# A four-layer decoder on one core: maxima turned and picked on chip in the fifth sublayer, and forty blocks of later keys and values among its first forty units

## The chip, the core and the metric

The kernel runs on one core of one Trainium2 chip, as one launch. The metric is the device time of that launch in microseconds (us), taken as the median of several runs. The engines are named as the profile names them: PE is the matrix engine (PEld its weight loads), DVE the vector engine, ACT the scalar engine, POOL the GpSimd engine, and SP the queue that issues nearly all DMA transfers. Each engine works through its own instructions in a fixed order and waits on semaphores for the others.

## What is computed

The reference is a decoder of four layers with three sublayers each, on 64 sequences of 64 tokens with 256 features (4096 tokens), all in f32. After each sublayer the result is added to x and normalized. Two sublayers bear on the change. The fifth is a cross attention with eight features to a head:

```python
# x and context, 64 x 64 x 256, are taken as 64 sequences of 8 heads x 8 rows x 256 columns
qk = einsum('bhdq,bhdl->bhql', qh, kh) * scale      # scores
sm = softmax(qk, axis=-1)
ret = einsum('bhql,bhdl->bhdq', sm, vh)
x = layernorm(x + gamma * ret)
```

The softmax needs the maximum of each row of scores. The eleventh sublayer is a cross attention whose keys and values are products of the context with two weights of 256x512; the context is an input, so these products depend on nothing that the earlier sublayers compute:

```python
k = (context @ Wk + bk)     # 4 heads of 128
v = (context @ Wv + bv)
```

## The kernel before

The tokens are held on chip as 32 tiles of 128 tokens in eight groups of four (TG = 4). The sublayers run one after the other; `self.ring` is a ring of eight weight slots of 1 MB each that all of them draw on in order.

**The fifth sublayer** is `l1_xattn`. It walks the 32 tiles in 34 steps, and each step in four units, one for each j, so there are 136 units. A unit has two halves, each a call of `scored`. In a step, `new` is the tile whose scores are formed for the first time, only to find the row maxima, and `old` is the tile two steps behind, whose scores are formed again, transposed, and go through the exponential. In a half, PE computes for `old` two banks `sk` and for `new` one tile `sq`. The operands of these products have 32 rows and lie in four groups of 32 partitions, two for `new` and two for `old`; the profile shows them as 32\*128. DVE takes the negated maxima of `sq` into `mc` (L1563). The maxima of `old` are brought into the banks `sk` ahead of the scores by a product with ones (L1551), so that the exponential on ACT (L1569) has nothing to subtract. `weighted` then multiplies the exponentials `e` with the values `vt` (L1600): the first half of a unit is followed by the second part of the unit two back, and the second half by the first part of the unit one back. The banks `sk` come from a ring of three, on which also the blocks `kv` and the turned maxima `mt` draw; the tiles `e` come from a ring of ten.

**The maxima's way.** After the first unit of a step, `move(turn)` deals with the tile whose maxima were finished in the step before. PE turns `mc` (L1575), ACT copies the high part (L1577), DVE forms the low part (L1578), SP writes both to DRAM (L1580) and reads two rows of each group of partitions back into `mx` (L670). `scored` needs `mx` at the start of the following step.

**The later keys and values.** `ContextRows` holds a list of blocks: one for the keys and one for the values of each chosen tile. `fill(n)` takes the next n blocks: two products of 128x128 by 128x512 on PE (L170; the profile shows four instructions), one copy of 128x512 on ACT (L174) and one write of 256 KB to DRAM on SP (L175). Before, 19 tiles are chosen, so there are 38 blocks: ten in the first ten units of the fifth sublayer, in whose code their results take a tile of the ring `e`; 21 around the end of the eighth sublayer; seven at the start of the ninth, in `Linear.first` (`fill(5)` and `fill(2)`). In the eleventh sublayer (`l3_xattn`), `ready` tells whether a tile was chosen. If so, its keys and values are loaded from DRAM and get their bias on POOL; otherwise PE forms them (L2143) and DVE adds the bias (L2604). The order of work on PE, DVE, ACT and POOL there is written out by hand in `l3_attentions`, together with the twelfth sublayer's.

**The sixth sublayer's weights.** `first.load()` takes four ring slots and loads three weights of 1 MB. Before, it stands ahead of the loop over the steps. From unit 48 on, one part of the list `ahead` runs in each unit: thirteen parts that form signs (POOL and DVE), seven that quantize the first group's rows, and then `first.turn`, with products and transposes of 128x128 on PE (L268, L273).

**Other parts of the stage.** `load` brings in a tile's operands, 1 MB in eight transfers, at the end of a step for the step after the next one. `store` writes results; after the last tile of a group four parts of `later` follow: a reciprocal and a scaling on DVE (L1634, L1635), loads, sums on POOL, and a normalization whose statistics are on DVE (L582, L585).

## Time and profile before

Three runs took 4292.81, 4290.98 and 4278.38 us; the median is 4290.98 us. The execution that was profiled took 4279.01 us, of which its span, from the first instruction to the last, is 4277.3 us.

| stretch of the span, us | what runs | length | PE busy | DVE busy | ACT busy | POOL busy | granted clock |
|---|---|---|---|---|---|---|---|
| 641 to 684 | fifth sublayer, units 0 to 9 | 43 | 34.48 | 27.81 | 15.23 | 9.35 | 0.87 |
| 684 to 817 | units 10 to 39 | 133 | 129.69 | 79.02 | 76.02 | 16.95 | 0.54 |
| 817 to 1239 | units 40 to 135 | 422 | 418.09 | 257.99 | 245.39 | 109.42 | 0.53 |
| 1934 to 1990 | end of the eighth, start of the ninth | 56 | 46.49 | 41.10 | 32.31 | 4.07 | 0.98 |
| 3250 to 4277 | eleventh and twelfth | 1027 | 951.99 | 737.82 | 651.61 | 394.43 | 0.99 |

### The profile page before, as it was taken

To read this page: it belongs to the slowest core of one execution; us is meant where nothing else is said; L and a number is where in the kernel's file an instruction comes from. 1 tells how busy PE (TensorE), PEld (TensorE's weight loads), DVE (VectorE), ACT (ScalarE), POOL (GpSimd) and SP (SyncE) were. 2 spreads that over 40 slices of the span, in tenths; PEclk is the share of its full clock that TensorE was granted. 3 is DMA by queue.
4 is the path that set the end of the run, shared out by engine and by line. 5 is a ranking of instruction groups with operands and counts; after the bars stand their busy time and mean duration, and the time that the engine had idled before them with its cause. 6 is when DMAs were issued, how large, how long until landed. Compare 5 with 4: busy or idle time off the path is not lost.

```text
span 4277.3 us, 71626 instructions
## 1 busy us (share of the span) xinstructions
PE 4044.9 (95%) x27272; PEld 2584.3 (60%) x27272; DVE 2988.3 (70%) x5646; ACT 2299.4 (54%) x4649; POOL 1549.7 (36%) x1617
## 2 busy tenths in 40 slices
PE   8879888999999899998999999999999989999997
PEld 6646664444457555554666666666666667666765
DVE  6856655676658468887777777777766777777775
ACT  5545454565543456755444444444443466676765
POOL 4511121141234111112555555555554343444432
PEclk9989996555579999999999999999999999999999
DMA  2211213434330000013111111111112110010000
GB/s 82 71 54 45 60 53 112 130 106 132 93 88 1 12 1 1 1 42 102 31 26 28 28 26 31 26 30 26 26 31 87 55 31 27 24 29 22 27 25 13
DMA packets 137307, 195.60 MB, mean 46 GB/s; under 512 B 22464, under 2 KB 89728, under 8 KB 135552
## 3 DMA queue, kind: packets, MB, share of 16 engines
q1 hardware_dynamic: 136000, 189.41, 16.0%
q8 instruction: 217, 3.56, 0.3%
q10 hardware_dynamic: 960, 1.57, 0.2%
q14 instruction: 130, 1.06, 0.1%
HBM read 100.47 MB, written 48.23 MB: 35 GB/s over the span
## 4 chain that ended last, share of the span: by engine, by line
PE 39%; DVE 9%; ACT 2%; issue 1%; POOL 1%; DVEq 0%; POOLq 0%; ACTq 0%
PE p L2143 18%; PE acc L2500 5%; PE acc L2766 4%; PE qT L562 2%; PE s L2438 2%; PE kT L562 1%; PE h L450 1%; PE y L2468 1%; PE yt L562 1%; DVE s L2699 1%; PE s L2692 1%; PE o L503 1%; PE pt L562 1%; DVE mxx L2701 1%; DVE s L2698 1%
## 5 line engine op out<-in xcount | busy, mean ns | idle before, releaser
L1563 DVE TENSOR_REDUCE mc<-sq 128x4 f32<-128x1024 f32 x256 | 310.8, 1222 | 174.6 <-PE sq L1558 161.4
L1569 ACT ACTIVATE e<-sk 128x512 f32<-128x512 f32 x512 | 278.1, 595 | 225.3 <-PE sk L1561 222.8
L556 POOL TENSOR_TENSOR rstd<-rstd,neg_half 128x1 f32<-128x1 f32 (+1 forms) x187 | 145.5, 778 | 588.0 <-DVE rstd L554 582.7
L556 POOL TENSOR_TENSOR hrq<-hrq,neg_half 128x4 f32<-128x4 f32 (+1 forms) x192 | 234.4, 1221 | 244.4 <-DVE hrq L554 238.2
L1600 PE MATMUL ret<-e,vt 128*32 128x256 f32 x2048 | 267.7, 616 | 1.4 <-ACT r L1605 1.4
L556 POOL TENSOR_TENSOR hrk<-hrk,neg_half 128x4 f32<-128x4 f32 x160 | 187.8, 1174 | 223.4 <-DVE hrk L554 173.7
L2143 PE MATMUL p<-l3a_wq,xt 128*128 128x512 f32 x512 | 243.8, 599 | 9.7 <-DVE v L543 8.4
L2143 PE MATMUL p<-l3a_wk,xt 128*128 128x512 f32 x512 | 247.9, 607 | 0.0
L2143 PE MATMUL p<-l3x_wq,xt 128*128 128x512 f32 x512 | 243.8, 599 | 0.8 <-DVE k L2604 0.8
L2766 PE MATMUL acc<-l3x_wo,yt 128*128 128x256 f32 x1024 | 235.0, 382 | 5.0 <-DVE yt L2750 3.5
L2143 PE MATMUL p<-l3a_wv,xt 128*128 128x512 f32 x512 | 233.2, 598 | 0.6 <-DVE k L543 0.4
L2500 PE MATMUL acc<-l3a_wproj,yt 128*128 128x256 f32 x1024 | 232.1, 379 | 0.7 <-DVE yt L543 0.7
L2500 PEld LDWEIGHTS acc<-l3a_wproj,yt 128*128 128x128 f32 x1024 | 194.2, 190 | 53.9 <-issue 29.2
L2766 PEld LDWEIGHTS acc<-l3x_wo,yt 128*128 128x128 f32 x1024 | 192.6, 191 | 40.8 <-ACT yt L2750 4.9
L1551 PE MATMUL sk<-mx,ones 2*128 2x512 f32 x512 | 201.1, 765 | 8.4 <-DMA mx<-l1x_m 6.6
L1558 PE MATMUL sq<-l1x 32*128 32x256 f32 x1024 | 191.4, 473 | 6.0 <-DVE mc L1563 5.8
L1551 PEld LDWEIGHTS sk<-mx,ones 2*128 2x128 f32 x512 | 73.5, 274 | 191.7 <-ACT e L1569 106.1
L562 PEld LDWEIGHTS qT<-ident,q 128*128 128x128 f32 x1024 | 121.5, 141 | 103.6 <-issue 76.4
L1561 PEld LDWEIGHTS sk<-l1x 32*128 32x128 f32 x1024 | 163.8, 315 | 19.7
L2484 POOL TENSOR_TENSOR hry<-hry,neg_half 128x8 f32<-128x8 f32 x64 | 106.2, 1659 | 179.1 <-DVE hry L2480 176.8
L562 PE MATMUL qT<-ident,q 128*128 128x128 f32 x1024 | 156.7, 276 | 11.7 <-DVE hlo L414 10.2
L1561 PE MATMUL sk<-l1x 32*128 32x256 f32 x1024 | 159.3, 401 | 0.0
(451 smaller groups left out, 10697.5 us busy)
## 6 DMA issues: line engine op xcount, KB each, us to landing
vs<-v SPq DMA_DIRECT2D x308, 128.0 KB
l1x<-l1x_c SPq DMA_DIRECT2D x128, 128.0 KB
l1x<-l1x_x SPq DMA_DIRECT2D x128, 128.0 KB
l3x_kv<-kv SPq DMA_DIRECT2D x38, 256.0 KB
k<-l3x_kv SPq DMA_DIRECT2D x19, 256.0 KB
v<-l3x_kv SPq DMA_DIRECT2D x19, 256.0 KB
x<-in_x SPq DMA_DIRECT2D x8, 512.0 KB
ct<-in_ctxT SPq DMA_DIRECT2D x8, 512.0 KB
```

The lines of the kernel that those rows point to most:

```text
L556: nc.gpsimd.tensor_tensor(out, out, self.neg_half[:, :n], ALU.pow)
L562: self.nc.tensor.transpose(ps[:, j * P : (j + 1) * P], blk, self.ident)
L1551: nc.tensor.matmul(ps, ones[rows], mx[old % 2][rows, j, :].unsqueeze(1).broadcast_to([2, 2, D]), start=True, stop=False)
L1558: nc.tensor.matmul(sq[:, k, n, :], x_[rows, j, part], c_[rows, j, :], start=True, stop=True)
L1561: nc.tensor.matmul(ps[:, n, :], c_[rows, j, part], x_[rows, j, :], start=False, stop=n == 1)
L1563: nc.vector.tensor_reduce(mc[new % 2][:, ra : ra + 2, 2 * j : 2 * j + 2], sq, AX.X, ALU.max, negate=True)
L1569: nc.scalar.activation(es[rb + k], ps, AF.Exp, scale=scale)
L1600: nc.tensor.matmul(ret[32 * r : 32 * r + 32, :], vt[i % 2][:, lc, 4 * j + r, :], es[r][:, lc, :], start=lc == 0, stop=lc == 1,)
L2143: self.nc.tensor.matmul(ps, lhs(c), w(c, cols), start=c == 0, stop=c == 1 and bias is None)
L2484: nc.gpsimd.tensor_tensor(r, r, self.neg_half[:, :8], ALU.pow)
L2500: nc.tensor.matmul(acc[:, :D], yts[h % 2][:, h // 2, :], wp[n // 8][:, (n % 8) * D : (n % 8 + 1) * D], start=n == 0, stop=n == 15,)
L2766: nc.tensor.matmul(acc[:, :D], yts[h % 2][:, h // 2, :], w.o[n // 8][:, (n % 8) * D : (n % 8 + 1) * D], start=n == 0, stop=n == 15,)
```

## The change

The maxima stay on chip. After the first unit of a step, DVE copies `mc` into the first eight columns of `mh` (rounded to the form that PE reads in one pass) and writes what was lost by the rounding into the next eight; PE turns `mh`, and ACT copies the result to `mt`. In `scored`, four products of 32 rows by 256 columns, two for each bank, take the place of two products of two rows by 512 columns: `pick` holds ones in the rows that belong to one column of maxima, so the product adds the high and the low part. The transfers through DRAM go, four for each tile. Of the later keys and values 31 tiles are chosen, all but the first, so there are 62 blocks: 40 in the first 40 units of the fifth sublayer, 21 around the end of the eighth as before, and one at the start of the ninth. `first.load()` moves into unit 41, as one of its slots is that of the blocks' weight; the list `ahead` is filled there and still starts at unit 48.

```diff
--- before.py
+++ after.py
@@ -148,7 +148,7 @@
     def __init__(self, dec):
         self.dec = dec
         tiles = [(g, t) for g in range(dec.n_groups) for t in range(TG)]
-        tiles = [tile for k, tile in enumerate(tiles) if k >= 3 and (k % 2 or k % 6 == 2)]
+        tiles = tiles[1:]
         self.dram = {}
         for g, t in tiles:
             for i in range(2):
@@ -1512,21 +1512,24 @@
         both = [self.weight(f"l1x{i}", F32R).rearrange("p (i n) -> p i n", i=2) for i in range(NB)]
         xr, cr = ([w[:, i].rearrange("p (j c) -> p j c", j=4) for w in both] for i in range(2))
         vt = [wk.tile([P, 2, 16, 32], F32, tag=f"vt{i}", name="vt", bufs=1) for i in range(2)]
-        mc = [wk.tile([P, 4, 32], F32, tag=f"mc{i}", name="mc", bufs=1) for i in range(2)]
-        mx = [wk.tile([P, 4, D], F32R, tag=f"mx{i}", name="mx", bufs=1) for i in range(2)]
-        ones = wk.tile([P, P], F32R, tag="ones", name="ones", bufs=1)
-        nc.scalar.activation(ones, self.ident, AF.Identity, bias=1.0, scale=0.0)
+        mc = [wk.tile([P, 4, 8], F32, tag=f"mc{i}", name="mc", bufs=1) for i in range(2)]
+        mh = [wk.tile([P, 4, 32], F32R, tag=f"mh{i}", name="mh", bufs=1) for i in range(2)]
+        mt = [wk.tile([P, P], F32R, tag=f"mt{i}", name="mt", bufs=1) for i in range(2)]
+        rows_of = wk.tile([P, 8], F32, tag="rows_of", name="rows_of", bufs=1)
+        pick = wk.tile([P, 8, P], F32R, tag="pick", name="pick", bufs=1)
+        of = self.ident.rearrange("p (r k n) -> p n r k", r=4, k=4)
+        nc.vector.tensor_reduce(rows_of, of[:, :, :, :2], AX.XY, ALU.add)
+        nc.gpsimd.tensor_copy(pick, rows_of.unsqueeze(2).broadcast_to([P, 8, P]))
         for t in vt:
             nc.gpsimd.memset(t, 0.0)
             nc.gpsimd.memset(t[:, :, :, 8:9], 1.0)
-        for t in mc:
-            nc.vector.memset(t, 0.0)
+        for t in mh:
+            nc.gpsimd.memset(t.bitcast(F32), 0.0)
 
         dram = lambda name, shape: [
             self.tc.dram_tile(shape, F32, name=f"l1x_{name}{g}") for g in range(self.n_groups)
         ]
         rd, sd, qd = (dram(n, [NTOK, D]) for n in "rsq")
-        md = [[self.tc.dram_tile([P, P], F32, name=f"l1x_m{h}{i}") for i in range(NB)] for h in range(2)]
         state = {}
 
         def load(g, t):
@@ -1544,13 +1547,15 @@
             for k in range(2):
                 if old is not None:
                     sks.append(bank("sk"))
-            group = lambda r, n=32: slice(32 * r, 32 * r + n)
+            group = lambda r: slice(32 * r, 32 * r + 32)
             ra, rb = 2 * half, 2 - 2 * half
-            for k, ps in enumerate(sks):
-                rows = group(rb + k, 2)
-                nc.tensor.matmul(
-                    ps, ones[rows], mx[old % 2][rows, j, :].unsqueeze(1).broadcast_to([2, 2, D]), start=True, stop=False
-                )
+            for n in range(2):
+                for k, ps in enumerate(sks):
+                    rows = group(rb + k)
+                    nc.tensor.matmul(
+                        ps[:, :, n * P : (n + 1) * P], pick[rows, 2 * j + n, :],
+                        mt[old % 2][rows].unsqueeze(1).broadcast_to([32, 2, P]), start=n == 0, stop=False,
+                    )
             for n in range(2):
                 part = slice(n * P, (n + 1) * P)
                 for k in range(2 if sq is not None else 0):
@@ -1571,17 +1576,12 @@
 
         def move(i):
 
+            m, h = mc[i % 2], mh[i % 2]
+            nc.vector.tensor_copy(h[:, :, :8], m)
+            nc.vector.tensor_tensor(h[:, :, 8:16], m, h[:, :, :8].bitcast(F32), ALU.subtract)
             ps = bank("mt")[:, 0, :P]
-            nc.tensor.transpose(ps, mc[i % 2].rearrange("p r n -> p (r n)"), self.ident)
-            hi, lo = (wk.tile([P, P], F32R, tag=tag, name=tag, bufs=1) for tag in ("mhi", "mlo"))
-            nc.scalar.copy(hi, ps)
-            nc.vector.tensor_tensor(lo, ps, hi.bitcast(F32), ALU.subtract)
-            for h, mt in enumerate((hi, lo)):
-                nc.sync.dma_start(out=md[h][i % NB], in_=mt.bitcast(F32))
-                self.load(
-                    mx[i % 2][h:P:32].bitcast(F32).rearrange("r j q -> r (j q)"),
-                    md[h][i % NB].rearrange("(r n) q -> r (n q)", r=4)[:, : 8 * P],
-                )
+            nc.tensor.transpose(ps, h.bitcast(F32).rearrange("p r n -> p (r n)"), self.ident)
+            nc.scalar.copy(mt[i % 2], ps)
 
         def values(g, t):
             v = vt[t % 2]
@@ -1661,8 +1661,7 @@
         load(*tiles[1])
         engines = {mybir.EngineType.PE, mybir.EngineType.Activation, mybir.EngineType.DVE}
         before, behind, turn, wait, units = None, None, None, 0, 0
-        first.load()
-        ahead = first.weights() + first.quantize(0) + [lambda: first.turn(0, bank("xt"), bank("rows"))]
+        ahead = []
         with self.tc.manual_schedule(engines=engines):
             for step in range(n + 2):
                 new = step if step < n else None
@@ -1680,7 +1679,7 @@
                     if before is not None:
                         weighted(*before, 0)
                     behind = before
-                    if units < 10:
+                    if units < 40:
                         self.context.fill(
                             1, wk, "e", 10, 0, nc.scalar.copy, lambda: bank("kv").rearrange("p i n -> p (i n)")
                         )
@@ -1692,6 +1691,10 @@
                             later.pop(0)[1]()
                             wait = 0
                     units += 1
+                    if units == 42:
+                        first.load()
+                        ahead += first.weights() + first.quantize(0)
+                        ahead.append(lambda: first.turn(0, bank("xt"), bank("rows")))
                     if units > 12 * TG and ahead:
                         ahead.pop(0)()
                     before = (old, j, es) if old is not None else None
```

## The prediction

> **What bounds the kernel now.** PE is busy 95% of the span, so I look for where its time is dear. The page's rows by slices, with the busy times above them:

> ```profile
> PE 4044.9 (95%) x27272; PEld 2584.3 (60%) x27272; DVE 2988.3 (70%) x5646; ACT 2299.4 (54%) x4649; POOL 1549.7 (36%) x1617
> ...
> PEclk9989996555579999999999999999999999999999
> ```

> The clock is halved in slices 6 to 10: the fifth sublayer, 641 to 1239 us. The answer by stretches (columns as in the front) shows PE full there, at half clock:

> ```profile
> 850.00:900.00 50.00, 50.00 (x417) 24.27 (x409) 35.89 (x44) 29.46 (x56) 28.82 (x23) 0.50 0.43 120
> ...
> 950.00:1000.00 50.00, 46.09 (x463) 23.76 (x461) 34.16 (x31) 32.57 (x63) 6.69 (x10) 0.73 0.52 138
> ```

> In 950 to 1000 the clock was high for a while. PE's timeline there:

> ```profile
> 966.49 0.64 PE L1600 MATMUL ret<-e,vt 128*32 128x256 f32 x8
> 967.05 0.68 PE L1551 MATMUL sk<-mx,ones 2*128 2x512 f32 x2
> ...
> 968.48 0.61 PE L1551 MATMUL sk<-mx,ones 2*128 2x512 f32 x2
> ...
> 972.89 0.50 PE L1551 MATMUL sk<-mx,ones 2*128 2x512 f32 x2 [2.69 <-DMA mx<-l1x_m]
> ```

> and in the steady state:

> ```profile
> 861.63 0.79 PE L1551 MATMUL sk<-mx,ones 2*128 2x512 f32 x2
> ...
> 863.79 0.79 PE L1551 MATMUL sk<-mx,ones 2*128 2x512 f32 x2
> ```

> A half takes 2.16 us at half clock, 1.42 at full. A step of eight halves and the turning (0.41 us, 1030.16 to 1030.57) takes 17.69 or some 11.7. The maxima's way through DRAM took 12 us (turned at 960.75, there at 972.89): hidden at half clock, late by 2.69 us at full. That wait costs the clock: by slices of 3.4 us it is 1.00 up to 973.3 and 0.50 after it; at 693.4, behind a wait of 2.47 us on the same transfer, it falls too. It came back at 949.4, when `first.turn` had sent products of 128x128 through PE.

> **An area count** (mine, from the rows) fits these turns. A 32x128 product fills a quarter of the array, one of 128x32 too. A 256-column pass takes 0.11 us at full clock in the scores; the f32 instructions of L170 take 0.43 for 512 columns (17.43 us for 40), which I count as two passes. A half then holds 512 array columns of scores and 1024 of `ret`; a window of 3.41 us has 8190. Windows at full clock that kept it held 0.38 or more, those that lost it 0.37 or less; the steady half clock holds 0.26 to 0.34 and never recovers; the lowest that recovered held 0.40. So I put the limit at 0.37 to 0.40.

> [...]

> **Units 0 to 9:** ten blocks as before; the wait of 1.48 us on `mx` at 672.85 goes. **-1.5.**

> **Units 10 to 39**, 30 blocks more. Before: two units from 683.91 to 693.40, then seven steps of 17.69: 133.3 us. After, four passes of 429 ns in each unit keep the area above 0.4, so the clock stays full. The unit's length shows in unit 10 of before, which follows two units with blocks:

> ```profile
> 676.93 0.27 PE L1575 MATMUL mt<-ident,mc 128*128 128x128 f32 x1
> ...
> 683.91 0.50 PE L1551 MATMUL sk<-mx,ones 2*128 2x512 f32 x2
> ...
> 685.95 0.50 PE L1551 MATMUL sk<-mx,ones 2*128 2x512 f32 x1 [0.30 <-ACT e L1569]
> ...
> 687.18 0.61 PE L1551 MATMUL sk<-mx,ones 2*128 2x512 f32 x2
> ```

> It takes 3.27 us: with five tiles of `e` in a unit and ten in the ring, the first `e` of a unit takes the place of the one two units back, which PE reads only after this half, so ACT's exponentials wait for PE and PE's next bank for ACT. Behind that ACT wait stand only exponentials that are not ready either. The block adds 1.82 (675.11 to 676.93), the turning 0.26 in seven steps: 30 x 5.09 + 1.8 = 154.5. **+21.** ACT's added copy (585 ns) fits into 5.1 us; if not, PE waits for banks.

> **Units 40 to 135.** The turning now waits for DVE: the last maxima come from the previous step, but DVE's copy and difference stand behind the reduce of the half just run. Steady row:

> ```profile
> 1028.00 0.79 PE L1551 MATMUL sk<-mx,ones 2*128 2x512 f32 x2
> ...
> 1030.16 0.48 PE L1575 MATMUL mt<-ident,mc 128*128 128x128 f32 x1
> ```

> ```profile
> 1029.07 1.22 DVE L1563 TENSOR_REDUCE mc<-sq 128x4 f32<-128x1024 f32 x1 [0.94 <-PE sq L1558]
> 1030.97 0.29 DVE L1578 TENSOR_TENSOR mlo<-mt,mhi 128x128 fp32r<-128x128 f32 x1 [0.68 <-ACT mhi L1577]
> ```

> The reduce ends at 1030.29; `sq` now follows two passes of `pick` instead of lying beside one, 0.21 later. The two small DVE operations aren't in the trace: the nearest are 128x4 ones, which follow each other by 0.21 when dependent (929.99, 930.20); 0.46 with the signal to PE. So PE turns at 1030.96 instead of 1030.16: 0.8 lost, in 23 steps **+18**. Bounds: nothing if the two are issued free of the reduce, 1.2 each (+28) if each takes the 0.29 of L1578 and more. Everything behind the turning on PE waits; ACT is then idle.

> At full clock the same wait is 1.2 us (0.66 + 0.57 of PE against 0.78 + 1.22 + 0.46 of DVE). A window holding it has (3.41 - 1.2 - 0.26) / 1.42 halves, each now 1792 columns with `pick`'s 256, and 256 of the turning: 0.33; split over two windows 0.37 to 0.43. By phase about one step in four falls below the limit. Group parts on DVE (1.73 + 0.45 us at 1048.87, 2.3 us at 1008.20) against a slack of some 0.9 (a reduce ends 0.67 + 1.22 after its half begins, and its tile is needed after two halves, 2.84) break it more surely; the first, for group 1, is in unit 44. So I expect the full clock to last about five units past the fill, 1.4 us each (4.32 less 2.9): **-7.** After `first.turn` in unit 68 it returns for seven or eight units, as before. At half clock `pick` lifts the area to at most 0.36, short of 0.37.

> `pick` itself: bounds 0 (same columns; weight loads run ahead) and 0.1 to 0.2 for a half (one weight load, 181 ns at full clock): 0 to +40. I take 0, as the weight loads of L1561 lie beside matmuls. Making `pick`, `rows_of` and `mh` lies beside units 0 to 7. `first.load()` in unit 41 has seven units before its data is used; 3 MB at the 300 GB/s and more of 1246 to 1254 us need 10. It is queued ahead of tile 12's load, which has a step of 17 us. SP loses 128 transfers of the maxima, which nothing else waits for.

> **Start of the ninth:** six blocks fewer. PE's fifth ended at 1980.21, when the scaled rows were ready since some 1979.5: -0.7; but PE is emptier, and a further window at half clock costs up to 1.7. **+1.**

> **Eleventh sublayer:** twelve tiles less to form, 3.44 us of PE each. Between first score products (L2692), a prepared tile followed by a prepared one takes 29.3 us (tiles 13, 14, 19, 20, 26), an unprepared one 29.8 (12, 18, 22, 28), a prepared one followed by an unprepared 30.65. So each tile saves 1.8, not 3.44: the values' part gives nothing. POOL's added sums fit in (20 of 50 us busy). **-21**, bounds 0 and -41.

> **Sum:** -1.5 + 21 + 18 - 7 + 1 - 21 = +10.5 on 4279.0: 4290. The runs' median, 4291.0, lies 12 above this execution, of which I add half: **4296**.

> **Rivals.** *The clock holds past unit 40* because no transfer is waited for. For: 949 to 973 kept it through seven windows, and `pick` adds area. Against: the wait for DVE above. A step then takes 8 x 1.42 + 0.26 + 1.2 = 12.8 against 17.7; throughout, 23 x 4.9 = 113, in place of +18 - 7: 4171. Held half the way: about 4235. *The clock falls between the blocks*: in units 10 to 39 a `kv` copy waits on ACT for its tile's write (SP issues eight loads at 0.59 and, every fourth step, eight more writes ahead of it), PE stops for lack of banks, and a window without a block falls under 0.37. It decides once that wait exceeds about 1 us; a unit then takes 4.32 + 3.6, 2.8 more; in ten units +28: 4324. *The change moves less than it says*: the 22 blocks left are the 21 near the eighth's end and one more, so no.

> **Chances.** Forecast 0.50 (4275 to 4312), the clock holding 0.27 (4165 to 4265), falling 0.23 (4305 to 4340). A measurement tells 0.3% (13 us) from no change. Faster: 0.27 and 0.04 of the forecast; same: 0.31 of it; slower: 0.15 and 0.23. The range leaves out a tenth at each end: 4235 to 4326.

> **What would show it.** Right: units 10 to 39 at clock 1.0 and 5.1 us; half clock again from about unit 45; PE's turning waiting 0.8 us for DVE; tiles of the eleventh at 29.3. Wrong: a granted clock above 0.8 from 840 to 1180, or below 0.9 before; a turning without a wait.

## The result and the profile after

The changed kernel takes **4320.35 us** (median of four runs, 4307.69 to 4337.39), the kernel before 4284.68 in the runs beside them: a ratio of 1.0091, 95% interval 1.007 to 1.0112, slower by 36 us. The prediction was 4296 in a range of 4235 to 4326. The profiled execution took 4307.69 us, the fastest of the four; its span is 4306.0, 28.7 more than before's 4277.3. The prediction's +10.5 answers to these 28.7. Here and below a ratio leaves out runs that lie more than 1.5% above the fastest run of the same kernel (two of e8's four, one of e10's ten), while the medians keep them. The changed kernel's page, the rows that were shown of before:

```profile
PE 4002.1 (93%) x27764; PEld 2581.6 (60%) x27784; DVE 2989.1 (69%) x5653; ACT 2310.9 (54%) x4672; POOL 1581.4 (37%) x1644
...
PEclk9989999956659999999999999999999999999999
```

The clock is at 0.9 or more in two slices that stood at 0.6 and 0.5 before, PE is busy for 43 us less, and yet the span is longer: PE now waits. By stretches of the fifth sublayer (units 0 to 9, 10 to 39, 40 to 135; columns as in the front):

```profile
641.00:682.60 41.60, 31.10 (x166) 13.86 (x160) 28.37 (x40) 15.05 (x28) 8.29 (x14) 0.88 0.37 119
682.60:850.10 167.50, 147.89 (x1332) 69.92 (x1331) 79.78 (x85) 90.25 (x173) 19.92 (x24) 0.99 0.40 124
850.10:1276.80 426.70, 400.67 (x3824) 211.92 (x3827) 259.86 (x316) 244.87 (x462) 109.08 (x111) 0.57 0.39 110
```

Between the starts of units (of the last stretch up to unit 135, without the 4.3 us of that unit):

| part | before | after | difference | predicted |
|---|---|---|---|---|
| units 0 to 9 | 42.7 | 41.9 | -0.8 | -1.5 |
| units 10 to 39 | 133.4 | 167.5 | **+34.1** | +21 |
| units 40 to 135 | 416.7 | 422.4 | +5.7 | +18 - 7 |
| unit 135 to the eleventh's first score product | 2033.8 | 2034.1 | +0.3 | +1 |
| from there to the first one of tile 31 | 938.6 | 927.4 | **-11.2** | -21 |
| the rest (ahead of unit 0, and the tail) | | | +0.7 | |

**Units with a block** run at full clock, as foretold, but at 5.58 us instead of 5.09. One of them, timeline of the changed kernel:

```profile
779.05 1.02 PE L170 MATMUL kv<-l3x_wkv,ct 128*128 128x512 f32 x2
...
780.67 0.64 PE L1600 MATMUL ret<-e,vt 128*32 128x256 f32 x8
...
781.38 0.59 ACT L174 COPY kv<-kv 128x512 f32<-128x512 f32 x1 [2.93 <-PE ret L1600]
781.86 1.09 ACT L1574 ACTIVATE e<-sk 128x512 f32<-128x512 f32 x2
...
782.02 0.88 PE L1555 MATMUL sk<-mt,pick 32*128 32x256 f32 x3 [0.71 <-ACT kv L174]
```

The block's products end at 780.07, its copy starts at 781.38, 0.07 after `ret` has ended: its tile of the ring still held exponentials that `ret` reads. Meanwhile the bank stays full and PE waits 0.71. Nine of the 30 copies wait so, all 1.3 us behind their products. They are only a part of it: the 21 units whose copy comes in time take 5.53 on the average too. PE's waits over all 30 units (us in total, times, longest):

```profile
PE sk L1555 <- ACT kv L174: 7.7, 15, 0.7
PE sk L1555 <- ACT e L1574: 5.6, 13, 0.6
PE ret L1600 <- ACT r L1605: 4.6, 15, 0.4
```

The unit that the forecast was read from has the second of these waits (0.30), but neither the first nor the third, which stands in every second unit.

**The turning** waits for DVE, as foretold, 0.65 at half clock:

```profile
890.82 1.22 DVE L1568 TENSOR_REDUCE mc<-sq 128x4 f32<-128x1024 f32 x1 [0.94 <-PE sq L1563]
...
891.96 0.17 DVE L1580 CAST mh<-mc 128x32 fp32r<-128x32 f32 x1
892.17 0.32 DVE L1581 TENSOR_TENSOR mh<-mc,mh 128x32 fp32r<-128x32 f32 x1
892.63 0.45 PE L1583 MATMUL mt<-ident,mh 128*128 128x128 f32 x1 [0.65 <-DVE mh L1581]
```

Steps at half clock take 18.3 instead of 17.7. In unit 52 the wait is far longer, since a group's statistics, themselves waiting for POOL's sum, stand between on DVE:

```profile
908.75 0.43 DVE L582 BATCH_NORM_STATS2 bnst<-z 128x6 f32<-128x256 f32 x1 [2.65 <-POOL z L1648]
...
911.70 2.34 DVE L1568 TENSOR_REDUCE mc<-sq 128x4 f32<-128x1024 f32 x2
...
914.74 0.45 PE L1583 MATMUL mt<-ident,mh 128*128 128x128 f32 x1 [4.39 <-DVE mh L1581]
```

**In the eleventh** the steady tiles take 29.3 as foretold, but tile 0 takes 35.60 instead of 31.43. Among the waits of these 35.6 us are POOL's for the prepared keys of tile 1 to arrive and PE's for POOL (us in total, times, longest):

```profile
POOL k L2600 <- DMA k<-l3x_kv: 9.3, 1, 9.3
PE yt L562 <- POOL y L2489: 3.9, 1, 3.9
```

The second row, of the same answer, is what PE loses: 0.3 before. On POOL that `y` comes behind the sums for tile 1's keys and values.

### The profile page after: what moved, and what is told of

Its sections match the earlier page's. It is cut to its first block, busy times and chain, and to the rows that moved or that the text cites. A ratio compares the mean times of both kernels' runs of the same rounds, so it can differ in the third digit from the quotient of the medians.

```text
span 4306.0 us, 72512 instructions
## 1 busy us (share of the span) xinstructions
PE 4002.1 (93%) x27764; PEld 2581.6 (60%) x27784; DVE 2989.1 (69%) x5653; ACT 2310.9 (54%) x4672; POOL 1581.4 (37%) x1644
## 3 DMA queue, kind: packets, MB, share of 16 engines
q14 instruction: 129, 1.06, 0.1%
## 4 chain that ended last, share of the span: by engine, by line
PE 57%; DVE 17%; ACT 7%; issue 3%; POOL 2%; DMA 1%; SPq 0%; ACTq 0%; POOLq 0%; DVEq 0%
PE p L2146 16%; PE acc L2503 5%; PE ret L1600 4%; PE sk L1555 3%; PE acc L2769 3%; PE acc L1766 2%; DVE s L2702 2%; PE kv L170 2%; PE gate L1961 2%; PE s L2441 2%; PE qT L562 2%; PE up L1961 2%; PE sk L1566 1%; PE kT L562 1%; PE acc L1977 1%
## 5 line engine op out<-in xcount | busy, mean ns | idle before, releaser
L1600 PE MATMUL ret<-e,vt 128*32 128x256 f32 x2048 | 233.8, 543 | 7.2 <-ACT r L1605 7.2
L1555 PEld LDWEIGHTS sk<-mt,pick 32*128 32x128 f32 x1024 | 117.8, 258 | 189.8 <-ACT e L1574 94.9
L1555 PE MATMUL sk<-mt,pick 32*128 32x256 f32 x1024 | 191.2, 434 | 18.2 <-ACT kv L174 8.7
L1563 PE MATMUL sq<-l1x 32*128 32x256 f32 x1024 | 167.5, 420 | 7.5 <-DVE mc L1568 7.3
L2146 PEld LDWEIGHTS p<-l3a_wv,xt 128*128 128x128 f32 x512 | 92.1, 190 | 97.4 <-issue 82.0
L2417 POOL TENSOR_TENSOR k<-k,hrk 128x512 f32<-128x512 f32 x128 | 144.7, 1130 | 10.0
```

The lines of the kernel that those rows point to most:

```text
L1555: nc.tensor.matmul(ps[:, :, n * P : (n + 1) * P], pick[rows, 2 * j + n, :], mt[old % 2][rows].unsqueeze(1).broadcast_to([32, 2, P]), start ...
L1563: nc.tensor.matmul(sq[:, k, n, :], x_[rows, j, part], c_[rows, j, :], start=True, stop=True)
L1600: nc.tensor.matmul(ret[32 * r : 32 * r + 32, :], vt[i % 2][:, lc, 4 * j + r, :], es[r][:, lc, :], start=lc == 0, stop=lc == 1,)
L2146: self.nc.tensor.matmul(ps, lhs(c), w(c, cols), start=c == 0, stop=c == 1 and bias is None)
L2417: nc.gpsimd.tensor_tensor(k, k, wide(r, P), ALU.mult)
```

## The experiments

"Half" is the time at half clock between unit 10 and the start of unit 135, from the clock records of the profiled execution; 516.7 us before. The stretches are of the one execution that was profiled, the ratio is to the kernel before, run beside each; where two kernels are compared below, it is by what each differs from its own runs of before.

| kernel | median, us | ratio, 95% interval | units 10 to 39 | units 40 to 135 | half | eleventh |
|---|---|---|---|---|---|---|
| changed | 4320.35 | 1.0091, 1.0070 to 1.0112 | 167.5 | 422.4 | 367 | 927.4 |
| e1 turning only | 4296.49 | 1.0042, 1.0029 to 1.0054 | 124.4 | 439.8 | 520 | 938.7 |
| e2 blocks only | 4321.98 | 1.0103, 1.0086 to 1.0120 | 180.4 | 417.5 | 414 | 927.7 |
| e3 DVE's part first | 4233.29 | 0.9909, 0.9880 to 0.9937 | 174.2 | 337.4 | 147 | 927.3 |
| e4 own tiles | 4306.30 | 1.0065, 1.0048 to 1.0082 | 148.5 | 425.9 | 377 | 927.5 |
| e5 both mends | 4193.34 | 0.9780, 0.9757 to 0.9803 | 148.0 | 330.3 | 96 | 927.6 |
| e6 e3 with ten blocks | 4168.57 | 0.9712, 0.9676 to 0.9749 | 94.8 | 364.9 | 219 | 938.5 |
| e7 23 tiles | 4304.21 | 1.0048, 1.0030 to 1.0066 | 142.3 | 443.6 | 491 | 933.3 |
| e8 parts spread | 4220.20 | 0.9777, 0.9723 to 0.9832 | 94.7 | 419.7 | 402 | 941.0 |
| e9 full products | 4410.99 | 1.0294, 1.0276 to 1.0312 | 174.0 | 523.7 | 476 | 924.2 |
| e10 narrow products | 4306.17 | 1.0056, 1.0033 to 1.0079 | 174.0 | 374.2 | 75 | 924.3 |
| e11 e6 with bursts | 4142.63 | 0.9666, 0.9647 to 0.9685 | 97.5 | 314.0 | 34 | 941.8 |
| e12 bursts in the wait | 4238.38 | 0.9888, 0.9869 to 0.9908 | 175.2 | 353.5 | 85 | 924.1 |

### e1 and e2: each part alone

e1 keeps the turning and picking and takes before's tiles, blocks and place of `first.load()`; e2 the reverse.

> The first part of the change alone: maxima turned and picked on chip; 19 tiles, ten blocks and the load of the sixth's weights as before. Theory (the blocks are what costs: units 10 to 39 took 34.1 us more in the changed kernel, units 40 to 135 only 5.6): a step at half clock takes 18.3 instead of 17.7 because PE's turning waits 0.6 for DVE, about 25 such steps are +16, the statistics' wait in unit 52 is +4, stretches that come back to full clock (two of 27 us in the changed kernel) take about 20 off, units 0 to 9 give 1.5: within 10 us of the kernel before, the eleventh unchanged. Rival (the turning is what costs, by its wait and by the clock lost with it): 20 us or more above before.

> The second part alone: 31 tiles, 40 blocks in the first 40 units, the sixth's weights loaded in unit 41; maxima through DRAM as before. Theory: units 10 to 39 take 165 to 170 us instead of 133, and the eleventh gives 11: +22 to +26 over before. The blocks' clock may be lost at the start of steps where the maxima come late, which adds some us. Rival (the turning is what costs): units 10 to 39 at most 145 us and a total at or below before.

e1 is 16 us above before, between its two cases: units 10 to 39 gain 9, as the clock is up from unit 10 to unit 21, units 40 to 135 lose 23: the wait at the turning, and of the stretches that come back to full clock only 3.4 us. e2 is 41 above, more than foretold: the clock falls seven times among its blocks, and units 10 to 39 take 180.

The maxima aren't late there: in these units PE never waits for `mx`, but 9.6 us for the blocks' copies, 4.6 for those of `ret` and 4.0 for exponentials, much as in the changed kernel. What e2 lacks is `pick`. Its products with ones have two rows instead of 32, and by the prediction's area count the seven windows ahead of the falls hold 0.25 to 0.37, while all but one of those that kept the clock hold 0.36 or more.

So the blocks are the larger cost and the turning costs by itself too. Together they cost less (36) than the sum of both (57). Of these 21 us 18 lie in units 40 to 135, where e1 loses 23, e2 1 and the changed kernel 6: its clock comes back twice, for 27 us each time, that of e1 once, for 3.4, and behind `first.turn` not at all.

### e3 and e4: the two waits taken away

```diff
+                    if j == 0 and turn is not None:
+                        parted(turn)          # the DVE copy and difference of move()
                     es = scored(new, old, j, 0)
```

> The changed kernel with DVE's copy and difference of the maxima issued ahead of the unit's first half instead of behind the reduce of its second: they are done two halves before PE turns them. Theory: the turning waits no more, a half-clock step takes 17.7 again (-0.65 in some 18 steps, -12), and at full clock the 1.2 us stop goes, so that the clock stays up for longer after unit 40 and after unit 68; each further step at full clock gives 5: 4230 to 4300. Rival (other stops, of the statistics on DVE and of the copy on ACT that is behind the blocks' copies, take the clock anyway): 4303 to 4310, with the same stretches at half clock.

```diff
-                            1, wk, "e", 10, 0, nc.scalar.copy, ...
+                            1, wk, "kv", 2, 0, nc.scalar.copy, ...
```

> The changed kernel with two tiles of their own for the blocks' results, so that these no longer share the ring of ten with the exponentials. Theory: the blocks' copies wait no more for a tile that the values' product still reads (1.3 us each in ten of 30 units) and the first exponential of a unit neither; units 10 to 39 take 140 to 150 us instead of 167: 4295 to 4305. Rival (ACT's and PE's own work, 5 us in a unit, is the bound, not the ring): 160 us or more and a total within 6 us of the changed kernel.

e3 takes 83 us off the changed kernel. DVE's two instructions run two halves ahead of the turning, which waits for nothing (timeline of e3):

```profile
1002.67 0.18 DVE L1580 CAST mh<-mc 128x32 fp32r<-128x32 f32 x1
...
1002.89 0.19 DVE L1581 TENSOR_TENSOR mh<-mc,mh 128x32 fp32r<-128x32 f32 x1
...
1005.37 0.33 PE L1587 MATMUL mt<-ident,mh 128*128 128x128 f32 x1
```

Once `first.turn` has raised the clock at 992.5 it stays up to the end of the stage, in steps of 12.2 to 12.8 us. Its first gain, half-clock steps of 17.7, is there too. The rival falls.

e4 takes units 10 to 39 to 148.5, 4.95 for a unit, 19 less than the changed kernel: the ring was the wait, and the rival (ACT's and PE's own work) falls. In its timeline the copy starts 0.08 after the products, and PE's next bank is free in time:

```profile
825.58 1.02 PE L170 MATMUL kv<-l3x_wkv,ct 128*128 128x512 f32 x2
...
826.68 0.59 ACT L174 COPY kv<-kv 128x512 f32<-128x512 f32 x1 [1.45 <-issue]
...
827.76 0.56 PE L1555 MATMUL sk<-mt,pick 32*128 32x256 f32 x2
```

The blocks alone are still not free: 148.5 is 15 more than before's 133.4. The whole kernel gains less: the medians, each against its own before, differ by 10 us only, and 4306 lies just above the 4295 to 4305 foretold. The profiled execution of e4 was its fastest, 13 below its median.

### e5 and e6: both mends, with 40 blocks and with ten

> The changed kernel with both edits: DVE's part of the maxima ahead of the unit's first half, and two tiles of their own for the blocks. Theory (the ring of tiles costs 15 in the blocks' units, and with no stop at the turning the clock that the blocks hold up stays up after them): units 10 to 39 take 148, and units 40 to 135 go on at some 12.3 for a step instead of 18.3, all the way if no other stop takes the clock (4150 to 4190), or up to the statistics in unit 52 and again from unit 68 (4190 to 4225). Rival (only `first.turn` in unit 68 can raise the clock for long; what follows the blocks falls whatever the turning does): the sum of the two single edits, 4215 to 4235.

> The first part alone (19 tiles, ten blocks, the sixth's weights loaded at the start) with DVE's part of the maxima ahead of the unit's first half. Theory: without the stop at the turning the clock stays up after the ten blocks too, so thirty more blocks are not needed for it; at full clock a block costs the 1.8 of its products, thirty cost 54 and give 11 in the eleventh: about 40 below the kernel with both mends, 4105 to 4160 if the clock never falls, up to 4200 if it falls between units 20 and 68. Rival (the thirty blocks are what keeps the clock up): it falls within ten units after the last block and returns with `first.turn` in unit 68: 4200 or more.

e5 is 87 below before, at the edge of its second case: the clock stays up after the blocks until 852.5 and comes back for good at 958. e6 is 25 us below e5, though its eleventh is 11 longer: without the turning's wait ten blocks suffice to carry the clock from unit 2 to unit 53, and thirty more cost 53 in units 10 to 39. But e6 still loses the clock, at 820 and at 994 in the profiled execution, which was its slowest. Ahead of the first fall (timeline of e6) statistics and a sign stand on DVE between the reduces and the turning:

```profile
814.82 0.43 DVE L582 BATCH_NORM_STATS2 bnst<-z 128x6 f32<-128x256 f32 x1
...
817.15 0.68 DVE L212 SCALAR_TENSOR_TENSOR l_signs<-l_wg,below 128x512 bf16<-128x512 f32 x1
...
818.30 0.30 PE L1587 MATMUL mt<-ident,mh 128*128 128x128 f32 x1 [2.03 <-DVE mh L1581]
```

### e7: which of the twelve tiles pay

```diff
-        tiles = tiles[1:]
+        tiles = [tile for k, tile in enumerate(tiles) if k not in (0, 1, 2, 4, 6, 10, 16, 18, 24)]
...
-                    if units < 40:
+                    if units < 24:
```

> The changed kernel with 23 tiles instead of 31: of the twelve added ones only those in the middle of the eleventh's pairs of groups (12, 22, 28, 30) are kept, and 24 blocks run in the first 24 units. Theory: these four give some 7 of the 11 us that the twelve gave in the eleventh, so from the first score product of tile 0 to that of tile 31 it takes 929 to 933 (927.4 with 31 tiles, 938.6 with 19); sixteen blocks less in the fifth give 1.0 to 1.3 each: 4302 to 4310. Rival (each of the twelve gives the same): 935 us there, a total of 4307 to 4316.

933.3 there: four of the twelve tiles give 5.3 of the 11.2 us, slightly less than foretold and more than a third, so the rival falls. In the fifth sublayer e7 gains 25 us on the changed kernel in units 10 to 39 and loses 21 behind them, since `first.turn` doesn't bring the clock back there, as in e1. Tile by tile in the changed kernel, tiles 12, 22, 28 and 30 give 1.7 to 1.8 each, 16 and 24 give 0.9, 10 and 18 some 0.45, and 1, 2, 4 and 6 together 1.6 up to tile 9.

### e8: the group parts spread

The reciprocal one unit later, the statistics one tile to a unit; e6 otherwise.

```diff
-                    (4, lambda: inverted(g, sm)), (2, lambda: fetched(g)), (3, lambda: added(g)),
-                    (2, lambda: normalized(g)),
+                    (5, lambda: inverted(g, sm)), (1, lambda: fetched(g)), (2, lambda: added(g)),
+                    (2, lambda: measured(g, 0)), (1, lambda: measured(g, 1)), (1, lambda: measured(g, 2)),
+                    (1, lambda: normalized(g)),
```

> The kernel with DVE's part of the maxima first and ten blocks, and the group parts spread: the reciprocal of the sums one unit later, so that its load has landed, and the statistics of a group's four tiles one tile to a unit instead of 2.3 us in a row. Theory (the two stretches at half clock that were left, 72 and 154 us, were both begun by such a DVE part, when PE had to wait for a reduce behind it): with the parts spread the clock stays at 1.0 from unit 2 to the end of the stage, or falls for less than 60 us in all; steps of 12.2 to 12.8 throughout, 4085 to 4120. Rival (the signs that DVE forms from unit 48 on, 0.68 each, or the quantizing in units 61 to 67 take the clock as well): 4130 or more, with the fall between units 48 and 68.

A miss: the median is 49 above e6, its two fastest runs are some 17 above it on the average, and the profiled execution, the slowest of the four, has 402 us at half clock. The fall is neither where I nor where the rival put it. It comes at 782, because `normalized` is now later and the next group's copy on ACT waits for POOL behind it, with exponentials queued behind the copy and PE behind these (timeline of e8):

```profile
779.07 1.04 ACT L1309 CAST z<-x 128x1024 fp32r<-128x1024 f32 x1 [1.07 <-POOL x L1671]
780.02 1.08 ACT L1574 ACTIVATE e<-sk 128x512 f32<-128x512 f32 x2
...
780.66 0.39 PE L1555 MATMUL sk<-mt,pick 32*128 32x256 f32 x2 [1.29 <-ACT e L1574]
```

The same copy stops PE again (1.22 us) ahead of the fall at 922, behind which the clock stays at half for 280 us, to the end of the stage. The four runs of e8 lie 76 us apart (4170.06 to 4245.76). Perhaps what a run takes depends on whether such a stop falls into a window that it spoils; with one of them profiled, that isn't shown.

### e9 and e10: more work for PE

In each half from step 10 on, two products into the tile that the scores then overwrite; e10 has `:32` for both `:128` (the widths of the output's rows and of `pick`).

```diff
+            for k in range(2 if new is not None and new >= 10 else 0):
+                nc.tensor.matmul(sq[:128, k, 0, :], pick[:, 0, :128], pick[:, :2, :], start=True, stop=True)
```

> The changed kernel with work added that changes no result: in each half from step 10 on, two products of 128 rows by 128 columns over 256 elements, written into the tile that the scores then overwrite. Theory (the clock goes by the share of the array that is used, and the half-clock state of this stage is one of too little area): 512 array columns more in each half hold the area at full clock at 0.4 or more even with the turning's wait, so that the clock is 1.0 in nearly all of units 40 to 135; a step takes some 14.5 (8 halves of 1.63, the turning and its wait) instead of 18.3: 4220 to 4260, although PE has more to do. Rival (PE's being busy is what counts, and it is busy all the time): the clock stays at 0.5 and the products add 0.43 a half: 4370 to 4410.

> The control to the full products: the same two products in each half, of 128 rows by 32 columns instead of 128 by 128, so that they take PE as long but fill a quarter of the array. Theory (area): 128 array columns more in a half are not enough, units 40 to 135 stay at half clock as in the changed kernel or more, and a step takes 21 to 22: 4370 to 4410. Rival (the number of products or PE's busy time counts): the same as with the full products.

Here my theory fell, in both, and so did the rival, which fits e9 but foretold the same for e10: the full products leave the stage mostly at half clock (e9), the narrow ones, a quarter of the area, bring it back within 3 to 17 us of every fall (e10). The profiled execution of e10 was its fastest, 41 below its median. The clock granted over the whole span tells of the others: 0.948 to 0.964 in e10, 0.926 to 0.928 in e9, 0.926 to 0.937 in the changed kernel. So every run of e10 spends less time at half clock than any of the other two kernels, though most spend more than the 75 us of the table. It isn't the area. e9 and e10 at half clock, one half each:

```profile
899.75 0.80 PE L1553 MATMUL sq<-pick 128*128 128x256 f32 x2
900.48 0.58 PE L1557 MATMUL sk<-mt,pick 32*128 32x256 f32 x2
...
902.64 0.80 PE L1553 MATMUL sq<-pick 128*128 128x256 f32 x2
```

```profile
868.76 0.64 PE L1553 MATMUL sq<-pick 128*32 128x256 f32 x2
869.33 0.58 PE L1557 MATMUL sk<-mt,pick 32*128 32x256 f32 x2
...
871.49 0.64 PE L1553 MATMUL sq<-pick 128*32 128x256 f32 x2
```

The same columns stream, but the full pair takes 0.73, the narrow one 0.57; its two weight loads take 0.18 us in the trace, those of the full pair 0.50. A half takes 2.89 against 2.73, so in e9 the same stream is thinner. That suggests a **stream count**: each product counts the columns it streams, plain f32 ones twice (at full clock the products of L170 with 512 columns start 0.429 us apart in the changed kernel, bf16 ones of L1748 with as many 0.216), those with rounded operands once, as the scores and `pick` (e11, below: five products of 512 columns in 2.11 us at half clock). It takes a product as a quarter where four run side by side (the eight of `ret` start in two fours, 7 ns apart in a four, 0.24 us from four to four: before, 954.04 to 954.30); one alone counts whole, here even at a width of 32. For the scores and `ret` this is the area count; for the narrow products it is four times it. The products with two rows of before and e2 it takes as a quarter, which is far more than their area. By it the median window at half clock in units 40 to 135 holds 0.34 of the 8192 columns of full clock in the changed kernel, 0.33 in e9 and 0.35 in e10, where a tenth of the windows hold 0.38 or more. The 8192 are an estimate: at half clock two products of L170, 1024 columns each by this count, start 0.853 us apart (825.35 and 826.20 in the changed kernel), which makes 4096 in 3.41 us, and twice that at full clock.

### e11 and e12: bursts placed by the stream count

Five products ahead of the turning, in every second step on top of e6 (e11), in every step on top of the changed kernel (e12):

```diff
+            for _ in range(5):                # e11: if i % 2 == 0
+                nc.tensor.matmul(
+                    ps[:32].rearrange("p i n -> p (i n)"), pick[:, 0, :32], pick[:, :4, :], start=True, stop=True
+                )
```

> The kernel with DVE's part of the maxima first and ten blocks, with work added that changes no result: ahead of every second turning five products of 128 rows by 32 columns over 512 elements, 2560 streamed columns, into the bank that the turning then overwrites. Theory (the clock of a window of 3.41 us goes by the columns streamed in the window before, whatever part of the array they fill: counted so, a limit of 0.37 of the 8192 of full clock sorts all but 15 of 2967 windows of the runs so far; the area count misses 24 in the control alone): at half clock the burst takes 2.1 us, so that at least one of the windows it falls in passes the limit, and the clock is back at the first burst after each fall: no stretch at half clock after unit 12 longer than some 40 us (72 and 154 without it); bursts cost 16 x 1.1 = 17, some 60 to 70 us of half clock become 20 to 30: 4120 to 4150. Rival (the full clock comes back by other things, as `first.turn`'s wide products): stretches as long as without the burst, 4185 or more.

> The changed kernel, its order untouched (the turning still waits for DVE), with the same five products ahead of every turning, where PE otherwise waits 1.0 to 1.2 us for DVE at full clock. Theory (streamed columns): the wait is filled, so that the window stays above the limit, and a clock that fell is back within a step; units 40 to 135 run at some 13 a step instead of 17.8 on the average, 25 to 40 us of stretches at half clock remain from the statistics and the like; the blocks' steps pay 1.1 each: 4210 to 4270. Rival (what counts is that PE waits for DVE, or the narrow products of the control worked by being in each half): units 40 to 135 mostly at half clock, steps of 19 or more: 4320 to 4360.

Both rivals fall. In e11 the clock falls once after unit 10, at 827.7, and is back 34 us later, right behind the next burst (timeline of e11):

```profile
860.10 2.11 PE L1588 MATMUL mt<-pick 128*32 128x512 f32 x5
...
862.05 0.27 PE L1592 MATMUL mt<-ident,mh 128*128 128x128 f32 x1
...
862.25 0.39 PE L1555 MATMUL sk<-mt,pick 32*128 32x256 f32 x2
```

The row at 862.25 has 0.39 us where the half-clock rows of the same line have 0.58. e11 is the fastest kernel of the study: 139 us below before, with runs only 5 us apart. The fastest run of e6, 4140.09, is no slower; e6's other three take 4168 to 4187. e12 does 2560 columns of useless work in the very wait of the changed kernel (timeline of e12), and is 79 us faster than it, though DVE's part still ends 0.57 us after PE is ready to turn:

```profile
894.85 1.60 PE L1584 MATMUL mt<-pick 128*32 128x512 f32 x5
894.90 0.17 DVE L1580 CAST mh<-mc 128x32 fp32r<-128x32 f32 x1
895.11 0.31 DVE L1581 TENSOR_TENSOR mh<-mc,mh 128x32 fp32r<-128x32 f32 x1
896.29 0.27 PE L1588 MATMUL mt<-ident,mh 128*128 128x128 f32 x1
```

## Why the prediction was right or wrong

The direction and the stages were right, two terms mis-sized in the same direction, one the other way. The median lies outside the band of the forecast itself, 4275 to 4312, and inside that of the second rival, 4305 to 4340, though the falls of the clock that this rival rests on didn't come: that its number fits is luck.

- **Units 10 to 39: +21, measured +34.1.** The clock is at 0.99 as foretold. The step that failed is the unit's length, 5.09, which measured 5.58: I took it from one unit whose copy came in time and which has no copy of `ret`, and wrote that behind the waiting exponential "stand only exponentials that are not ready either". The block's copy is queued there too, and its own tile can be one that `ret` still reads. PE's waits for the blocks' copies (7.7) and for those of `ret` (4.6) make 12.3 us, against the 13 over the forecast. I had priced a late copy only as a rival, by its write to DRAM. e4 prices the ring at 19 of the 34, the exponentials' waits included; with tiles of their own the unit takes 4.95.
- **Units 40 to 135: +18 for the turning, measured 0.65 instead of 0.8 a step** at half clock, plus 3.7 in unit 52, where statistics on DVE come between. I had named these parts as breakers of the clock, not as a longer wait.
- **The full clock's stay: -7.** It fell at 854, in unit 40, sooner than the five units I gave it, because the late block's copy and a 1.05 us copy of a group's rows on ACT came together: PE waits 0.71 and 1.06 in one window. It came back after `first.turn` for 27 us, as foretold, and at 1072.5 by itself, which I had excluded: `pick` lifts the window's share to "at most 0.36", I wrote. By the stream count that one window held 0.37 to 0.38. So this term came out better than forecast: +5.7 in place of +11 with the turning's.
- **`pick` at 0: right.** A half at full clock takes 1.42 in e3 as before.
- **Start of the ninth, +1:** within the 0.3 of the whole stretch up to the eleventh.
- **Eleventh: -21, measured -11.2** (and 1.2 back in the tail). The 1.8 per tile is right for the tiles it was read from, in the middle of the pairs of groups, and I applied it to all twelve. Tiles 16 and 24, next to tiles that take some 33.7 us in both kernels, give half: what the tile ahead of them gains (1.75), they lose in part themselves (0.8). At the start tile 0 loses 4.2: PE waits 3.9 for POOL, whose prepared keys for tile 1 arrive late. That the load is the cause is likely, as tile 0 takes 32.44 in e7, where tile 1 isn't prepared, but it isn't shown apart from POOL's added sums.
- **From the profile to the median, +6:** the changed kernel's profiled run was its fastest, 13 below its median; before's was 6 below. The four runs of the changed kernel lie 30 us apart, at mean clocks between 0.926 and 0.937.

The first rival's mechanism was real, only not in this kernel: when the turning doesn't wait (e3, e5) the clock does hold for most of the stage (147 and 96 us at half), and e5's 4193 lies near the 4171 I gave it. Of the second, the place and the stop were right, and 4324 is near the median; but the clock fell for one window of 3.4 us only in units 10 to 39, and the copies waited for `ret` rather than for their writes.

PE's being busy did not tell the clock here: the stage stays at half clock in windows that the profile lists as fully busy (in before 50.00 of 50.00 us at 0.50, from 850 to 900). Nor did a fall take an idle window: 101 falls were seen, at shares of up to 0.43 by the stream count. One window of 3.41 us was enough for a change: in the changed kernel the clock falls at 823.4, behind one with a share of 0.31, and is back at 826.8, behind one with 0.45.

## What to carry to other kernels

Ask of each wait that a change adds not only how long it is but what it does to the clock of its window: here 1 us of DVE stood ahead of a 128x128 turning, and moving two 0.2 us instructions up by two halves in the same queue gained 83 us (e3), more than any other edit of the changed kernel alone. Work that is moved "under" another stage needs buffers of its own, for a shared ring turns it into a wait of the stage that lends them (e4: 19 us in that stage, 10 in the median). A saving per tile holds for the tiles it was read from (e7); read it at the ends as well before multiplying.

## What the runs showed of the chip

- **In these traces the clock went with a count of streamed columns.** In each of the fourteen traces every change of the clock between 640 and 1500 us lies on a grid of 3.41 us (in before and in the changed kernel each record of the clock there lasts 3.413 us or a multiple of it). Over 3461 such windows, at a limit of 0.37 of 8192 columns (the limit read from these windows, the 8192 estimated as under e10), the count of one window gave the clock of the next in all but some 20 (13 to 21, by how a product's columns are spread over its listed time). Of 114 rises 113 came at 0.37 or more, the lowest at 0.365; the highest share that stayed low was 0.375; 94 of 101 falls came below 0.37. Counted by area, 52 windows are wrong instead of 21, 24 of these in e10. Of the seven falls above the limit three lie at 0.37 to 0.38. The other four, at 0.40 to 0.43, are in before and e2 and hold the products with two rows: with these counted by their area, all four come to 0.37 or less. So in before and e2 a product of two rows seems to have counted little, in e10 to e12 a single one of 32 columns whole; no run was made to test the first.
- **Half clock was a trap in this stage.** With no stop at all its stream came to 0.35 of the window's columns at half clock (1792 in 2.16 us) and to 0.53 at full clock (1792 in 1.42 us), on either side of 0.37. The stage mostly stayed in the state it was in: at half clock from 693.4 to 949.4 and from 973.3 to 1239.6 in before, at full clock from 992.5 to its end in e3. A dense narrow stream of 2.1 us was enough to bring the clock back each time (once in e11, four times in e12's units 40 to 135).
- **Useless work was faster in one form and slower in another**: e12 adds 82 thousand streamed columns to the changed kernel and saves 79 us; e9 adds 90 thousand in pairs that take 0.73 us with 0.50 of weight loads (0.57 with 0.18 for e10's narrow ones), and costs 92.
